# Attention and two quantised convolutions on 16 images: one more image through the filtered convolution, a reordered last head, split loads

## The chip, the cores and the metric

The kernel runs on one core of a Trainium2 chip. The metric is the device time of one execution in microseconds (us). All times are medians of repeated executions, and all comparisons use runs in the fast state (granted TensorE clock 0.994 in every profile of this study); five experiments have a single run each, whose state cannot be told, and are read by their profiles alone.

## The reference, cut to what matters

x is 16 images of 128 channels and 32 x 32 positions, in f32. Layer 0 is attention with 4 heads over the 1024 positions, layer 1 two 3x3 convolutions on values quantised to 4 bits, each followed by a batch norm over all images.

```python
# layer 0
scores = jnp.einsum('bnc,bcm->bnm', q, k) * c ** (-0.5)     # 64 heads of 1024 x 1024
attn = jax.nn.softmax(scores, axis=-1)
out = jnp.einsum('bnm,bmc->bnc', attn, v)
x = einsum(out, w_out) + b_out + x
# layer 1
out = act_quant(x)                       # round(clip(x, 0, 1) * 15) / 15
out = conv3x3(out, weight_quant(w1))
out = batchnorm(out, gamma1, beta1)      # mean and variance over (0, 2, 3): needs all 16 images
out = act_quant(out)
out = conv3x3(out, weight_quant(w2))
out = batchnorm(out, gamma2, beta2)
return out + x
```

The batch norms cut the program into stages: nothing of the second convolution can start before the last rows of image 15 have left the first, and no output before the last rows have left the second.

## The kernel before

Some names first. PSUM is the memory in which TensorE's products land; it is split into banks, and each buffer of `ps_s`, `ps_a` or `ps_m` takes up one or two. `u` (in PSUM `psu`) is an image multiplied by the folded query and key weights; `vo` (`psv`) is one multiplied by the folded value and output weights, which `fold_b` (`ps_b`) makes from wvo. `pad` is a quantised image with a border. The aggregate is the VectorE instruction that makes mean and variance out of the statistics of single tiles.

The loop of layer 0 has 512 steps: 64 heads (16 images of 4) with 8 chunks of 128 keys. A step does the scores of one chunk (`pss`, 4 records of 0.43 us), the exponential on ScalarE, and one step later the product with the values (`psa`). Other work is hung on steps by `at(step, function)`. The value projections of the next image (`psv`) stand at two steps of each head:

```python
vp = pool("vo", NCH + 4)          # 12 buffers for the projected values, 8 to an image
ps_s = pool("ps_s", 2, space=PSUM)
ps_a = pool("ps_a", 1, space=PSUM)   # tags a0 and a1
ps_m = pool("ps_m", 2, space=PSUM)   # tag "mm": u, v, filtered products, first conv
# ... in the loop of steps:
                if j in (5, 6) and b + 1 < B:
                    project_v(b + 1, 2 * h + j - 5)
```

The first convolution of images 0 to 13 runs inside this loop in a filtered form: the padded image is turned into 16 tiles of sums and differences, each is multiplied by a transformed weight (16 products of 256 columns, in place of 18 products of 512), and the results are summed. `products` does 4 of the 16. Images 14 and 15 are convolved directly after the loop:

```python
            if b < B - 2:
                at(end + 4, quantize, b, xt, A_LEVELS, 0.0)
                for i in range(2):
                    at(end + 5 + i, transform_rows, b, i)
                    at(end + 7 + i, transform_columns, b, i)
                    at(end + 14 + i, products, b, i)
                    at(end + 17 + i, transform_columns, b, 2 + i)
                    at(end + 22 + i, products, b, 2 + i)
                at(end + 26, statistics, b, 0)
# ...
        at(n_steps - 1, first_conv, B - 1, 0, RPH - 1, 0)
        at(n_steps + 1, normalise_group, len(GROUPS) - 1)
        for hf in range(NHF):
            at(n_steps + 2, first_conv, B - 2, hf * RPH)
        at(n_steps + 2, first_conv, B - 1, RPH - 1, 8, 1)
        at(n_steps + 3, first_conv, B - 1, RPH + 7, 9, 2)
```

A direct convolution writes one PSUM tile, which ScalarE copies out and VectorE takes statistics of, in this order:

```python
        ps = pool.tile([P, rows, W], F32, tag=tag, name=f"psc{n}_{b}_{r}")
        # ... nine products, one for each tap
        nc.scalar.copy(ys[b][:, r * W : (r + rows) * W], ps)
        if group is not None:
            nc.vector.bn_stats(place(n, b, group), ps)
```

## Time and profile before

| | before |
|---|---|
| time, first three runs | 2132.03 us (2131.83 to 2134.93) |
| span of the profiled execution | 2130.7 us |
| TensorE busy | 98% |
| first scores start | 10.11 us |
| loop: first scores to last scores | 2007.07 us |
| tail: last scores to the first aggregate of the batch norm | 15.08 us |
| first aggregate to the first product of the second conv | 4.21 us |
| second conv, to its aggregate | 65.03 us |
| aggregate to the first output pass | 1.99 us |
| first output pass to the end | 27.21 us |

The six stages and the start add up to the span. This is the way to read this kernel: TensorE is busy everywhere except at the joints, and each part of the change works at one joint. Intervals between two named instructions of one trace repeat to some hundredths of a microsecond in most stages (the loop to 0.3, the start and the output to less than that, as shown below), while whole runs differ by 2 us and more.

### The profile page before, as it was taken

To read this page: it belongs to the slowest core of one execution; us is meant where nothing else is said; L and a number is where in the kernel's file an instruction comes from. 1 tells how busy PE (TensorE), PEld (TensorE's weight loads), DVE (VectorE), ACT (ScalarE), POOL (GpSimd) and SP (SyncE) were. 2 spreads that over 40 slices of the span, in tenths; PEclk is the share of its full clock that TensorE was granted. 3 is DMA by queue.
4 is the path that set the end of the run, shared out by engine and by line. 5 is a ranking of instruction groups with operands and counts; after the bars stand their busy time and mean duration, and the time that the engine had idled before them with its cause. 6 is when DMAs were issued, how large, how long until landed. Compare 5 with 4: busy or idle time off the path is not lost.

```text
span 2130.7 us, 14771 instructions
## 1 busy us (share of the span) xinstructions
PE 2089.5 (98%) x5265; PEld 938.9 (44%) x5266; DVE 1445.9 (68%) x2139; ACT 735.7 (35%) x848; POOL 6.8 (0%) x16
## 2 busy tenths in 40 slices
PE   9999999999999999999999999999999999999994
PEld 4444444444444444444444444444444444444541
DVE  4776666767677676667758666775766667675676
ACT  2333333333333333333333333333333333333355
POOL 0000000000000000000000000000000000000000
PEclk9999999999999999999999999999999999999997
DMA  1000000000000000000000000000000000000043
GB/s 61 12 20 0 0 20 1 20 0 10 10 0 20 0 20 0 0 20 0 20 1 20 0 0 20 0 20 0 20 0 0 20 1 10 0 5 6 1 168 159
DMA packets 10609, 36.81 MB, mean 17 GB/s; under 512 B 1440, under 2 KB 1568, under 8 KB 10528
## 3 DMA queue, kind: packets, MB, share of 16 engines
q1 hardware_dynamic: 9872, 33.76, 4.3%
q10 hardware_dynamic: 656, 2.03, 0.3%
q8 instruction: 43, 0.70, 0.1%
q14 instruction: 38, 0.31, 0.0%
HBM read 19.01 MB, written 16.78 MB: 17 GB/s over the span
## 4 chain that ended last, share of the span: by engine, by line
PE 91%; DVE 7%; ACT 1%; issue 0%; DMA 0%; ACTq 0%; DVEq 0%
PE pss L480 38%; PE psa L504 37%; PE psv L459 5%; PE psu L448 5%; PE psc L275 3%; PE psw L711 1%; DVE rb L562 1%; DVE part L527 1%; DVE av L573 1%; DVE es L515 1%; DVE acc L574 1%; ACT e L493 1%; PE psa L619 1%; DVE y L856 1%; DVE side L553 0%; DVE vo L467 0%
## 5 line engine op out<-in xcount | busy, mean ns | idle before, releaser
L480 PE MATMUL pss<-u,x 128*128 128x512 f32 (+1 forms) x2064 | 964.7, 589 | 0.0
L493 ACT ACTIVATE e<-pss 128x1024 f32<-128x1024 f32 x511 | 522.8, 1023 | 1251.9 <-PE pss L480 1215.7
L504 PE MATMUL psa<-e,vo 128*128 128x512 f32 x2016 | 947.7, 592 | 0.0
L515 DVE TENSOR_TENSOR es<-es,e 128x1024 f32<-128x1024 f32 x378 | 461.2, 1220 | 366.4 <-ACT e L493 364.3
L480 PEld LDWEIGHTS pss<-u,x 128*128 128x128 f32 x2064 | 389.9, 190 | 474.1 <-issue 454.4
L504 PEld LDWEIGHTS psa<-e,vo 128*128 128x128 f32 x2016 | 379.4, 190 | 460.6 <-issue 459.4
L467 DVE COPY vo<-psv 128x512 f32<-128x512 f32 x128 | 88.2, 689 | 212.5 <-PE psv L459 212.5
L448 PE MATMUL psu<-x,at_sb 128*128 128x512 f32 x256 | 130.9, 593 | 0.3 <-DVE at_sb L414 0.2
L459 PE MATMUL psv<-bt_sb,x 128*128 128x512 f32 x256 | 130.4, 592 | 0.0
L527 DVE TRANSPOSE_TENSOR_REDUCE part<-es 128x32 f32<-128x1024 f32 (+1 forms) x66 | 80.6, 1221 | 2.2
L562 DVE STREAM_TRANSPOSE rb<-sums 128x1024 f32<-128x1024 f32 (+1 forms) x66 | 80.0, 1212 | 1.8
L513 DVE TENSOR_TENSOR es<-e,e 128x1024 f32<-128x1024 f32 x63 | 76.7, 1217 | 0.0
L459 PEld LDWEIGHTS psv<-bt_sb,x 128*128 128x128 f32 x256 | 48.6, 190 | 61.2 <-issue 61.0
L448 PEld LDWEIGHTS psu<-x,at_sb 128*128 128x128 f32 x256 | 48.4, 190 | 61.5 <-issue 53.8
L275 PE MATMUL psc<-pad,wq 128*128 128x512 bf16 (+3 forms) x333 | 71.9, 377 | 0.6 <-DVE pad L250 0.6
L453 DVE TENSOR_SCALAR u<-psu,au_sb 128x512 f32<-128x512 f32 x64 | 47.8, 746 | 34.2 <-PE psu L448 34.2
L718 ACT COPY wino<-psw 128x512 f32<-128x512 f32 x112 | 61.3, 589 | 24.9 <-PE psw L711 24.9
L703 DVE TENSOR_TENSOR tiles<-rows 128x1024 bf16<-128x1024 bf16 x56 | 67.1, 1219 | 0.5
L573 DVE TENSOR_TENSOR av<-av,rb 128x1024 f32<-128x1024 f32 x47 | 57.5, 1223 | 2.2 <-ACT e L493 0.3
L574 DVE TENSOR_TENSOR acc<-acc,av 128x1024 f32<-128x1024 f32 x47 | 57.3, 1220 | 0.5
L275 PEld LDWEIGHTS <-wq 128*128 128x128 bf16 x333 | 32.2, 97 | 39.9 <-DVE pad L250 1.1
L520 ACT COPY av<-psa 128x512 f32<-128x512 f32 x63 | 36.9, 585 | 37.2 <-PE psa L504 37.2
(121 smaller groups left out, 736.2 us busy)
## 6 DMA issues: line engine op xcount, KB each, us to landing
x_dram<-x SPq DMA_DIRECT2D x16, 512.0 KB, 2.6
res<-x_dram SPq DMA_DIRECT2D x16, 512.0 KB, 9.6
x<-in_x_dram SPq DMA_DIRECT2D x15, 512.0 KB, 3.6
out_dram<-y SPq DMA_DIRECT2D x15, 512.0 KB, 4.8
raw<-in_cw_dram ACTq DMA_DIRECT2D x2, 576.0 KB, 3.6
wvo_sb<-in_wvo_dram ACTq DMA_DIRECT2D x1, 514.0 KB, 6.8
out_dram<-y SPq DMA_DIRECT2D x2, 256.0 KB, 2.0
wqk_sb<-in_wqk_dram SPq DMA_DIRECT2D x1, 385.5 KB, 6.8
```

Of the source, the lines that this page charges most:

```text
L275: last = nc.tensor.matmul(ps, lhsT=wq[n][:, tap, :], rhs=pads[b % NPAD][:, r + dy : r + dy + rows, dx : dx + W], start=(tap == 0), stop=(t ...
L448: nc.tensor.matmul(ps, lhsT=at_sb[:, h, :], rhs=xt[b][:, ts(hf, HALF)], start=True, stop=True)
L459: nc.tensor.matmul(ps, lhsT=xt[b][:, ts(j, P)], rhs=bt_sb.rearrange("p h o -> p (h o)"), start=True, stop=True,)
L467: nc.vector.tensor_copy(vos[b, j], ps)
L480: last = nc.tensor.matmul(ps[:, ts(m, N // len(parts))], lhsT=xt[b][:, ts(key, P)], rhs=us[g][:, queries], start=True, stop=True,)
L493: exps[:] = [nc.scalar.activation(e, ps, AF.Exp).ins]
L504: nc.tensor.matmul(psa[g][m], lhsT=vos[b, j][:, ts(h, P)], rhs=e[:, ts(m, HALF)], start=(j == 0), stop=(j == NCH - 1),)
L515: added = nc.vector.tensor_tensor(es[g], es[g], es.pop((g, j)), ALU.add)
L527: nc.vector.tensor_reduce(part, total.rearrange("p (k c) -> p k c", c=Q), AX.X, ALU.add, apply_transpose=True,)
L562: nc.vector.transpose(rb, rinv.unsqueeze(2).to_broadcast([P, n, Q]))
L573: nc.vector.tensor_tensor(av, av, rb, ALU.mult)
L574: nc.vector.tensor_tensor(accs[b], accs[b], av, ALU.add)
```

## The change

The intent: run image 14 through the filtered form too, so that less is left after the loop; issue filtered products behind the scores of their step; put the last head's last products ahead of image 15's first rows; load what is needed first, first; and make the pieces at the start of each stage smaller, so that the next engine starts earlier. The diff, cut:

```diff
 # (start) the loads
-        nc.scalar.dma_start(out=wvo_sb, in_=wvo)
-        nc.sync.dma_start(out=wqk_sb[:, 1:], in_=wqk[:, 1:])
-        load(1)
+        nc.sync.dma_start(out=wvo_sb[0 : P // 2], in_=wvo[0 : P // 2])
+        nc.scalar.dma_start(out=wvo_sb[P // 2 :], in_=wvo[P // 2 :])
+        # load_rest: the rest of wqk, bo, bnp behind the first u; image 1 behind the first exponential
 # (conv) statistics ahead of the copy, and behind the last quantising
-        nc.scalar.copy(ys[b][:, r * W : (r + rows) * W], ps)
         if group is not None:
-            nc.vector.bn_stats(place(n, b, group), ps)
+            with tc.issue_after(after) if after else nullcontext():
+                nc.vector.bn_stats(place(n, b, group), ps)
+        nc.scalar.copy(ys[b][:, r * W : (r + rows) * W], ps)
 # (products)
+                with tc.issue_after(scored[0]):
                     for i in range(2):
                         nc.tensor.matmul(ps[:, i], lhsT=wino[:, l, k + i, :], ...)
 # (loop) image 14 filtered as well, with tighter slots
-            if b < B - 2:
+            when = (11, 13, 15, 19) if b == B - 2 else (14, 17, 22, 26)
+                at(end + when[0] + i, products, b, i)
+                at(end + when[1] + i, transform_columns, b, 2 + i)
+                at(end + when[2] + i, products, b, 2 + i)
 # (tail) image 14's direct convs gone, image 15's rows behind the last products
-        at(n_steps - 1, first_conv, B - 1, 0, RPH - 1, 0)
-            at(n_steps + 2, first_conv, B - 2, hf * RPH)
+        at(n_steps + 2, first_conv, 0, RPH - 1, 0)
+        at(n_steps + 2, first_conv, RPH - 1, 8, 1)
+        at(n_steps + 3, first_conv, RPH + 7, 9, 2)
 # (second conv) pieces of image 0's quantising, and of the first and last image's rows
-        for r0, r1 in ((0, RPH + 1), (RPH + 1, H)):
+        for r0, r1 in ((0, 10), (10, RPH + 2), (RPH + 2, H)):
+        starts = {0: (0, 8, RPH, H), B - 1: (0, RPH, H - 8, H)}
 # (output) quarters and halves first, the first two passes on VectorE
-            parts = NHF if b == 0 else 1
+        parts = {0: (0, N // 4, N // 2, N), 1: (0, N // 2, N), 2: (0, N // 2, N)}
+                if b == 0 and hi <= N // 2:
+                    nc.vector.tensor_scalar(y, y, scale2, bias2, ALU.mult, ALU.add)
```

More of the change, by code (lines that the diff above doesn't have):

```diff
@@ L222, in fast_path @@
     nc.gpsimd.memset(ones, 1.0)
-    LATE = 2
     STATS = nc.vector.BN_STATS_DIM
-    early = [keep.tile([P, (B - LATE) * NHF, STATS], F32, name=f"early{n}") for n in range(2)]
+    early = [keep.tile([P, (B - 1) * NHF, STATS], F32, name=f"early{n}") for n in range(2)]
     late = [
-        keep.tile([P, 3 + (LATE * NHF + 1 - n) * STATS], F32, name=f"late{n}") for n in range(2)
+        keep.tile([P, 3 + 3 * STATS], F32, name=f"late{n}") for n in range(2)
     ]
     for n in range(2):
-        nc.gpsimd.memset(late[n][:, 0:1], float((B - LATE) * N))
+        nc.gpsimd.memset(late[n][:, 0:1], float((B - 1) * N))
     ys = [keep.tile([P, N], F32, name=f"y{b}") for b in range(B)]
@@ L258, in place @@
     def place(n, b, i):
-        if b < B - LATE:
+        if b < B - 1:
             return early[n][:, b * NHF + i, :]
-        k = 3 + ((b - B + LATE) * NHF + i) * STATS
+        k = 3 + i * STATS
         return late[n][:, k : k + STATS]
@@ L266, in gather, with conv @@
         nc.vector.tensor_scalar(
-            late[n][:, 2:3], late[n][:, 2:3], float((B - LATE) * N), None, ALU.mult
+            late[n][:, 2:3], late[n][:, 2:3], float((B - 1) * N), None, ALU.mult
         )
-    def conv(pool, tag, b, n, r, rows=RPH, group=None):
+    def conv(pool, tag, b, n, r, rows=RPH, group=None, after=None):
         ps = pool.tile([P, rows, W], F32, tag=tag, name=f"psc{n}_{b}_{r}")
@@ L282, in conv @@
         ps = ps.rearrange("p h w -> p (h w)")
+        if group is not None:
+            with tc.issue_after(after) if after else nullcontext():
+                nc.vector.bn_stats(place(n, b, group), ps)
         nc.scalar.copy(ys[b][:, r * W : (r + rows) * W], ps)
-        if group is not None:
-            nc.vector.bn_stats(place(n, b, group), ps)
         return last
@@ L371, in fast_path, with load @@
         xt, us, vos, es, avs, psa, accs = {}, {}, {}, {}, {}, {}, {}
-        exps, sums_added, scored = [], [], []
+        exps, sums_added, scored, attended, quantized = [], [], [], [], []
         heads = [(b, h) for b in range(B) for h in range(NH)]
-        def load(b):
+        def load(b, queue=nc.sync):
             xt[b] = xp.tile([P, N], F32, tag="x", name=f"x{b}")
-            nc.sync.dma_start(out=xt[b], in_=x[b])
+            queue.dma_start(out=xt[b], in_=x[b])
         wqk_sb = once.tile([P, NH, 2 * P + 1], F32, tag="rows", name="wqk_sb")
@@ L386, in fast_path, with load_rest @@
         nc.scalar.dma_start(out=xt[0][:, ts(1, HALF)], in_=x[0][:, ts(1, HALF)])
-        nc.scalar.dma_start(out=wvo_sb, in_=wvo)
-        nc.sync.dma_start(out=wqk_sb[:, 1:], in_=wqk[:, 1:])
-        load(1)
-        nc.sync.dma_start(out=bo_sb, in_=bo)
-        nc.sync.dma_start(out=bnp_sb, in_=bnp)
+        nc.sync.dma_start(out=wvo_sb[0 : P // 2], in_=wvo[0 : P // 2])
+        nc.scalar.dma_start(out=wvo_sb[P // 2 :], in_=wvo[P // 2 :])
+        def load_rest(behind):
+            with tc.issue_after(behind):
+                nc.scalar.dma_start(out=wqk_sb[:, 1:], in_=wqk[:, 1:])
+                nc.scalar.dma_start(out=bo_sb, in_=bo)
+                nc.scalar.dma_start(out=bnp_sb, in_=bnp)
         def warm_up(n):
@@ L454, in project_u @@
             else:
-                nc.scalar.activation(dst, ps, AF.Identity, bias=au_sb[:, h : h + 1])
+                copied = nc.scalar.activation(dst, ps, AF.Identity, bias=au_sb[:, h : h + 1])
+                if g == 0:
+                    load_rest(copied.ins)
         def project_v(b, j):
@@ L544, in inverse_sums @@
                 for i in range(w):
-                    nc.tensor.matmul(
+                    product = nc.tensor.matmul(
                         ps, lhsT=quad, rhs=part[:, ts(i, n)], start=(i == 0), stop=(i == w - 1)
                     )
+                attended[:] = [product.ins]
                 nc.vector.reciprocal(rinv, ps)
@@ L614, in attend_group @@
             for m, key in enumerate(keys):
-                with tc.issue_after(first_product.ins) if final and m else nullcontext():
-                    if final and m == 1:
+                if final and m == 3:
+                    with tc.issue_after(attended[0]):
                         rbs[i] = inverse_sums(LAST, quadrant_sums(total), slice(*GROUPS[i]))
+                with tc.issue_after(attended[0]) if final and m else nullcontext():
                     product = nc.tensor.matmul(
@@ L625, in attend_group @@
                     )
-                first_product = first_product if m else product
+                attended[:] = [product.ins]
             avs[i] = psa[LAST, i]
@@ L639, in normalise_group @@
             done = quantize(b, x1, A_LEVELS, 0.0, cut.start // W, cut.stop // W)
+            quantized[:] = [done.ins]
             if i == len(GROUPS) - 1:
                 nc.sync.dma_start(out=x1d[b], in_=x1)
-                behind.append(done.ins)
         later = {}
@@ L709, in products @@
                 ps = ps_m.tile([P, 2, D, D], F32, tag="mm", name=f"psw_{b}_{l}_{k}")
-                for i in range(2):
-                    nc.tensor.matmul(
-                        ps[:, i],
-                        lhsT=wino[:, l, k + i, :],
-                        rhs=tiles[b][:, l % 2, k + i],
-                        start=True,
-                        stop=True,
-                    )
+                with tc.issue_after(scored[0]):
+                    for i in range(2):
+                        nc.tensor.matmul(
+                            ps[:, i],
+                            lhsT=wino[:, l, k + i, :],
+                            rhs=tiles[b][:, l % 2, k + i],
+                            start=True,
+                            stop=True,
+                        )
                 nc.scalar.copy(m[:, k : k + 2], ps)
@@ L731, in products, with first_conv @@
                     nc.vector.tensor_tensor(y[..., c], y[..., c], e, op)
-        def first_conv(b, r, rows=RPH, group=None):
-            convs[:] = [conv(ps_m, "mm", b, 0, r, rows, group).ins]
+        def first_conv(r, rows, group):
+            with tc.issue_after(attended[0]):
+                attended[:] = [conv(ps_m, "mm", B - 1, 0, r, rows, group, quantized[0]).ins]
         def keep_clock():
@@ L740, in keep_clock @@
             flat = wq[0].rearrange("p t o -> p (t o)")
-            with tc.issue_after(convs[0]):
-                for _ in range(21):
+            with tc.issue_after(attended[0]):
+                for _ in range(16):
                     nc.tensor.matmul(
@@ L750, in preload, with load_second @@
             nc.scalar.activation(keep.tile([P, 1], F32, name="unused"), last[:, N - 1 :], table)
+        def load_second():
+            with tc.issue_after(exps[0]):
+                load(1, nc.scalar)
         def late_bn_constants():
@@ L754, in late_bn_constants @@
                 bn_constants()
-        behind, convs = [], []
-        def late_statistics():
-            with tc.issue_after(behind[0]):
-                statistics(B - 2, 0)
         n_steps = len(heads) * NCH
+        at(1, load_second)
         at(NCH + 4, lambda: constants(cleared.ins, sums_added[0]))
@@ L769, in fast_path @@
             at(end + 6, sums_range, b)
-            if b < B - 2:
-                at(end + 4, quantize, b, xt, A_LEVELS, 0.0)
-                for i in range(2):
-                    at(end + 5 + i, transform_rows, b, i)
-                    at(end + 7 + i, transform_columns, b, i)
-                    at(end + 14 + i, products, b, i)
-                    at(end + 17 + i, transform_columns, b, 2 + i)
-                    at(end + 22 + i, products, b, 2 + i)
-                at(end + 26, statistics, b, 0)
-            else:
-                at(end + 4, quantize, b, xt, A_LEVELS, 0.0)
-        at((LAST - 2) * NCH, gather, 0)
+            at(end + 4, quantize, b, xt, A_LEVELS, 0.0)
+            when = (11, 13, 15, 19) if b == B - 2 else (14, 17, 22, 26)
+            for i in range(2):
+                at(end + 5 + i, transform_rows, b, i)
+                at(end + 7 + i, transform_columns, b, i)
+                at(end + when[0] + i, products, b, i)
+                at(end + when[1] + i, transform_columns, b, 2 + i)
+                at(end + when[2] + i, products, b, 2 + i)
+            at(end + when[3], statistics, b, 0)
+        at(LAST * NCH - 2, gather, 0)
         for i in range(len(GROUPS) - 1):
             at(LAST * NCH + FIRST_STEP[i + 1] + 1, normalise_group, i)
-        at(n_steps - 1, first_conv, B - 1, 0, RPH - 1, 0)
         at(n_steps - 1, preload, AF.Sqrt)
         at(n_steps + 1, normalise_group, len(GROUPS) - 1)
-        for hf in range(NHF):
-            at(n_steps + 2, first_conv, B - 2, hf * RPH)
-        at(n_steps + 2, first_conv, B - 1, RPH - 1, 8, 1)
-        at(n_steps + 2, late_statistics)
-        at(n_steps + 3, first_conv, B - 1, RPH + 7, 9, 2)
+        at(n_steps + 2, first_conv, 0, RPH - 1, 0)
+        at(n_steps + 2, first_conv, RPH - 1, 8, 1)
+        at(n_steps + 3, first_conv, RPH + 7, 9, 2)
         at(n_steps + 3, keep_clock)
@@ L832, in fast_path @@
             x1.append(t)
-        for r0, r1 in ((0, RPH + 1), (RPH + 1, H)):
+        for r0, r1 in ((0, 10), (10, RPH + 2), (RPH + 2, H)):
             quantize(0, ys[0], scale1, bias1, r0, r1)
         quantize(1, ys[1], scale1, bias1)
+        starts = {0: (0, 8, RPH, H), B - 1: (0, RPH, H - 8, H)}
         for b in range(B):
-            for hf in range(NHF):
-                conv(ps_c, "c", b, 1, hf * RPH, group=hf if b == B - 1 else None)
+            rows = starts.get(b, (0, RPH, H))
+            for i, (r0, r1) in enumerate(zip(rows, rows[1:])):
+                conv(ps_c, "c", b, 1, r0, r1 - r0, group=i if b == B - 1 else None)
             if b + 2 < B:
@@ L845, in fast_path @@
                     check_sums()
-            if b == B - LATE - 1:
+            if b == B - 2:
                 gather(1)
         scale2, bias2 = bn_params(1)
+        parts = {0: (0, N // 4, N // 2, N), 1: (0, N // 2, N), 2: (0, N // 2, N)}
         for b in range(B):
-            parts = NHF if b == 0 else 1
-            for i in range(parts):
-                cut = ts(i, N // parts)
-                y = ys[b][:, cut]
-                nc.scalar.activation(y, y, AF.Identity, bias=bias2, scale=scale2)
-                nc.vector.tensor_tensor(y, y, x1[b][:, cut], ALU.add)
-                nc.sync.dma_start(out=out[b][:, cut], in_=y)
+            ends = parts.get(b, (0, N))
+            for lo, hi in zip(ends, ends[1:]):
+                y = ys[b][:, lo:hi]
+                if b == 0 and hi <= N // 2:
+                    nc.vector.tensor_scalar(y, y, scale2, bias2, ALU.mult, ALU.add)
+                else:
+                    nc.scalar.activation(y, y, AF.Identity, bias=bias2, scale=scale2)
+                nc.vector.tensor_tensor(y, y, x1[b][:, lo:hi], ALU.add)
+                nc.sync.dma_start(out=out[b][:, lo:hi], in_=y)
     outer.close()
```

## The prediction

> **What bounds the kernel now.** I read the page first, then the engines' windows, TensorE's list of waits, and the timeline of the first 24 us and of everything after 2000 us.
>
> ```profile
> PE 2089.5 (98%) x5265; PEld 938.9 (44%) x5266; DVE 1445.9 (68%) x2139; ACT 735.7 (35%) x848; POOL 6.8 (0%) x16
> ...
> PE 91%; DVE 7%; ACT 1%; issue 0%; DMA 0%; ACTq 0%; DVEq 0%
> ```
>
> TensorE is busy for 98% of the span and carries 91% of the chain that ended last. So time can come from two places only: columns that TensorE no longer streams, and the few stretches where it idles or does filler work. The windows say where those are:
>
> ```profile
> 0.00:10.00 10.00, 6.67 (x22) 4.35 (x23) 1.11 (x3) 1.97 (x2) 3.73 (x12) 1.00 0.74 255
> 500.00:1000.00 500.00, 498.35 (x1202) 221.58 (x1201) 343.57 (x500) 167.92 (x194) 0.00 (x0) 1.00 0.03 9
> 2100.00:2131.00 31.00, 0.11 (x1) 0.00 (x0) 20.77 (x25) 19.46 (x19) 0.00 (x0) 0.56 0.67 272
> ```
>
> (First number after the stretch: its length; second: TensorE busy.) The 500 us in the middle lose 1.65 us. The first 10 us lose 3.3, the last 31 nearly all. What TensorE waited for:
>
> ```profile
> PE psw L711 <- DVE vo L467: 6.6, 14, 0.5
> PE ps_b L420 <- DMA wvo_sb<-in_wvo_dram: 1.9, 1, 1.9
> ```
>
> The first is 0.47 us once for each of 14 filtered images: a product waits for a buffer that VectorE still copies out. The second is the start.
>
> **What the skill says, and whether the trace agrees.**
> - "TensorE: Matmul & The Clock Gate", Back-to-back issue gap: N/2.4 + 2.5 ns when warm. Four filtered products of 256 columns stand 0.43 us from the next group (204.80 to 205.24), 0.11 each; the formula's 0.109 agrees. An f32 product costs four times a bf16 one here: 512 columns take 0.86 us (two products, shown as four records, per 1.72 us).
> - "VectorE: DVE Perf Modes", What auto-detection actually checks: a one-source SBUF operation runs two elements a cycle only if the outermost dimensions are both even, or equal. It agrees: below, 17 image rows into the padded image took 0.72 us and 15 rows 0.66, while 16 rows took 0.43 and 32 rows 0.70.
> - "PSUM — Partial Sum Buffer", PSUM bank collisions: two engines may not touch one bank together, reads included, so they are ordered. It agrees: the statistics of a PSUM tile start only when ScalarE's copy of it ends.
> - "DMA: Bandwidth & Descriptors", Queues, rings and completion order: the DMA engines alternate between the two issuing engines' queues. It agrees: 514 KB of wvo alone on one queue needed 6.8 us to land, beside 385 and 512 KB on the other.
>
> **The change, part by part.** Times are on the clock of the profile before; negative is faster.
>
> 1. *Start.* These lines are the end of the loads:
>
> ```profile
> 7.24 0.69 ACT L455 ACTIVATE u<-psu,au_sb 128x512 f32<-128x512 f32 x1 [1.04 <-PE psu L448]
> 9.14 1.13 PE L420 MATMUL ps_b<-wvo_sb 128*128 128x128 f32 x8 [1.94 <-DMA wvo_sb<-in_wvo_dram]
> ```
>
> wvo is split over both queues; the 385 KB of other weights and image 1 move behind u. Landing shows about 0.7 us after the last bytes (x's first half landed at 4.65; the 0.39 MB up to it had moved by 3.9). So wvo's bytes were through near 8.3, and the one-us windows (181, 231, 330, 367, 384, 388, 308 GB/s from 2.0 us on) sum to 1.97 MB by then, of which fold_b needed 1.18: the first weights, image 0 and wvo. Those 1.18 MB are through near 6.3 when nothing else is queued, and land at 7.0 to 7.4. The product before it leaves TensorE near 6.95, so fold_b starts at 7.2: -1.9. But the order of the new kernel puts the scores of step 1 ahead of both psv products, which now stand next to each other, and the fold after them needs a buffer that VectorE frees 0.7 us after the first: +0.2. Estimate -1.7.
>
> 2. *Products behind the scores.* The instruction order on TensorE is identical for images 0 to 13: the products were already behind the scores of their step. The 6.6 us stay: 0.
>
> 3. *Image 14 filtered.* 16 products of 256 columns more, at 0.1075: +1.72, inside the loop where TensorE is the bound. VectorE gets some 17 us more over steps 486 to 501, with slots packed tighter. I walked its order with the durations of the list of groups (1.22 for a sum of 1024, 0.69 and 0.42 for the filter's sums): at the change of heads in the middle of it the copy of av comes some 1.5 us later than in other heads, and about 0.5 us before the next product wants its buffer. 0.
>
> 4. *The tail.*
>
> ```profile
> 2019.28 2.02 PE L275 MATMUL psc<-pad,wq 128*128 128x480 bf16 x9
> ...
> 2025.03 6.26 PE L275 MATMUL psc<-pad,wq 128*128 128x512 bf16 x36
> ...
> 2031.33 0.40 ACT L283 COPY y<-psc 128x288 f32<-128x288 f32 x1 [0.75 <-PE psc L275]
> 2031.76 0.47 DVE L285 BATCH_NORM_STATS2 late<-psc 128x6 f32<-128x288 f32 x1 [0.72 <-ACT y L283]
> 2032.26 0.30 DVE L311 BATCH_NORM_AGGREGATE mv<-late 128x2 f32<-128x33 f32 x1
> ```
>
> x36 is 18 products of image 14 (3.9 us) and 18 of image 15. Image 14's go. In the new order the last products of the last head follow the scores directly: four keys 2019.28 to 2021.0, three more to 2022.3. Then TensorE waits for VectorE's part (2022.61 plus 0.2), 0.4 of sums, 0.43 of last product: 2023.55. Image 15's rows take 1.82 + 0.97 + 1.09: 2027.43. Meanwhile VectorE normalises and quantises the last quarter, 1.9 us of it after the last product: done at 2026.1, just before the last rows want it (2026.34). Statistics no longer wait for ScalarE's copy: aggregate at 2028.2 instead of 2032.26. -4.0.
>
> 5. *Smaller first quantised piece.*
>
> ```profile
> 2035.21 0.44 DVE L249 TENSOR_SCALAR qt<-qt 128x544 f32<-128x544 f32 x1 [0.91 <-ACT qt L248]
> 2035.69 0.72 DVE L250 TENSOR_SCALAR pad<-qt 128x544 bf16<-128x544 f32 x1
> 2036.33 0.40 DVE L249 TENSOR_SCALAR qt<-qt 128x480 f32<-128x480 f32 x1
> 2036.45 2.37 ACT L248 ACTIVATE qt<-y,bias,scale 128x1024 f32<-128x1024 f32 x2 [0.59 <-DVE pad L250]
> ```
>
> 10 rows for 17: ScalarE 0.66 to about 0.48, VectorE 0.44 to 0.33, and, rows now even, 0.72 to 0.33. -0.68. The later pieces come 0.3 to 0.4 us ahead of their conv.
>
> 6. *Second conv's end.*
>
> ```profile
> 2100.15 0.58 ACT L283 COPY y<-psc 128x512 f32<-128x512 f32 x1 [1.34 <-PE psc L275]
> 2100.77 0.70 DVE L285 BATCH_NORM_STATS2 late<-psc 128x6 f32<-128x512 f32 x1 [1.23 <-ACT y L283]
> ```
>
> Statistics start 0.58 earlier and cover 256 columns (0.43 for 0.70): -0.84.
>
> 7. *Output.* The first transfer leaves 1.6 us after the bias; now two passes of 256 on VectorE (0.30 + 0.42), so 0.8 earlier. But from 2108 on the transfers run at 373 to 422 GB/s until 2127, four us behind VectorE. The small pieces feed 131 KB per 0.72 us, less than that rate, and half-images add at 0.70 per 256 KB, so most of the 0.8 is starved away: by my count of bytes -0.3.
>
> Sum: -1.7 + 1.72 - 4.0 - 0.68 - 0.84 - 0.3 = -5.8, from 2132.0: **2126.2 us**, 0.27%.
>
> **Rivals.**
> - *The 6.6 us go as well* (the title suggests it): 2119.6. The unchanged order speaks against it.
> - *VectorE falls behind in image 14's packed steps.* It is 68% busy overall and nearly full at 2000 to 2005 (4.96 of 5). If av or a filtered tile comes late, TensorE stalls 0.5 to 2 us: 2127 to 2128.
> - *Image 14's rows were cover.* They hid the last normalising; my margin without them is 0.2 us. A wait at the last rows would cost up to 1: 2127.
> - *Half a transfer per queue is no faster.* If 64 partitions reach only half the engines' rate, or three issues on ScalarE delay bt, the start gives 0.7 rather than 1.7: 2127.2.
> - *Output wholly bound by the transfers' start*: all 0.8 kept: 2125.7.
>
> **Range and chances.** Three of the rivals add about a us each; two subtract, the larger of them unlikely. Repeats of the kernel before differ by up to 3.1 us (2131.83 to 2134.93), though two of three agree in 0.2. 80%: 2123.5 to 2129.0. A move of 2% (43 us) has no source in 98% busy TensorE: faster 0.005, slower 0.005, within 0.99.
>
> **What would show it.** The profile after should have: fold_b near 7.2 without a wait over 0.3; the psw waits on vo still 14 times 0.47; 240 psw records against 224; no new TensorE wait between 1950 and 2000; last rows right behind the others, and the first conv's aggregate about 4 us nearer to the last scores; 10-row quantising near 0.33; VectorE's last statistics ahead of ScalarE's copy; and the span from the bias to the end shorter by 0.2 to 0.8. I am wrong if the psw waits vanish, if TensorE waits for pad or av, or if the end does not move with the tail.

## The result, and the profile after

| | before | after |
|---|---|---|
| median of 4 runs | 2132.21 us | 2128.36 us (2127.49 to 2129.32) |
| ratio | | 0.9979, 95% interval 0.9962 to 0.9997 |
| span of the profiled execution | 2130.7 us | 2125.7 us |

A ratio here is the mean time of one kernel's fast runs over that of the other's of the same rounds, so it is not quite the ratio of the medians. The change saves 0.2%: within 2%, as predicted, and 2.2 us above the predicted time. Stage by stage, in the profiles:

| stage | before | after | difference | predicted |
|---|---|---|---|---|
| first scores start | 10.11 | 8.80 | -1.31 | -1.7 |
| loop | 2007.07 | 2008.83 | +1.76 | +1.72 |
| tail | 15.08 | 11.86 | -3.22 | -4.0 |
| aggregate to second conv | 4.21 | 3.46 | -0.75 | -0.68 |
| second conv to its aggregate | 65.03 | 64.19 | -0.84 | -0.84 |
| aggregate to output pass | 1.99 | 1.97 | -0.02 | |
| output | 27.21 | 26.59 | -0.62 | -0.3 |
| span | 2130.7 | 2125.7 | -5.0 | -5.8 |

The list of what TensorE waited for, after (total us, times, longest; two lines left out, 1.1 for the first operands and 0.5 for `pad` at the start of the second convolution, which the kernel before has as well):

```profile
PE psw L719 <- DVE vo L472: 6.6, 14, 0.5
PE psc L273 <- ACT y L284: 0.6, 1, 0.6
PE ps_b L423 <- DMA wvo_sb<-in_wvo_dram: 0.5, 1, 0.5
PE psu L451 <- DMA x<-in_x_dram: 0.4, 1, 0.4
```

The first line is that of the kernel before, unchanged: the products "behind each step's scores" still wait 14 times, and image 14, the fifteenth filtered image, does not. The wait for wvo has shrunk from 1.9 to 0.5, at the price of 0.4 for x. The second line is new: a convolution waits for ScalarE's copy. The timeline of the kernel after shows where (start, duration, then the work; in brackets the idle time before it and what ended it):

```profile
2019.72 3.27 PE L626 MATMUL psa<-e,vo 128*128 128x256 f32 x14
2024.09 3.03 PE L273 MATMUL psc<-pad,wq 128*128 128x480 bf16 x18
2026.37 1.22 DVE L283 BATCH_NORM_STATS2 late<-psc 128x6 f32<-128x480 f32 x2
2027.06 0.94 ACT L284 COPY y<-psc 128x480 f32<-128x480 f32 x2 [4.18 <-DVE late L283]
2027.67 1.29 PE L273 MATMUL psc<-pad,wq 128*128 128x288 bf16 x9 [0.55 <-ACT y L284]
2028.99 0.47 DVE L283 BATCH_NORM_STATS2 late<-psc 128x6 f32<-128x288 f32 x1 [1.40 <-PE psc L273]
2029.49 0.25 DVE L310 BATCH_NORM_AGGREGATE mv<-late 128x2 f32<-128x21 f32 x1
2032.56 0.33 DVE L248 TENSOR_SCALAR pad<-qt 128x320 bf16<-128x320 f32 x1
2096.67 0.43 DVE L283 BATCH_NORM_STATS2 late<-psc 128x6 f32<-128x256 f32 x1 [0.55 <-PE psc L273]
2097.14 0.25 DVE L310 BATCH_NORM_AGGREGATE mv<-late 128x2 f32<-128x21 f32 x1
```

Read the first seven lines as a chain. The first conv tile is complete near 2026, but VectorE takes its statistics only at 2026.37, behind the last quantising; in this order ScalarE may copy the tile only behind the statistics, at 2027.06; and the third piece of image 15 (x9, 288 columns) needs the bank of the first, since "mm" has two. So it starts at 2027.67 instead of right behind the second piece. The eighth line is the small quantised piece (0.33, where 17 rows took 0.72), the last two the end of the second conv: the statistics no longer follow a copy, and the aggregate follows them at once.

### The profile page after: what moved, and what is told of

Same layout as the page of the kernel before. It is cut to its first block, busy times and chain, and to the rows that moved or that the text cites. A ratio compares the mean times of both kernels' runs of the same rounds, so it can differ in the third digit from the quotient of the medians.

```text
span 2125.7 us, 14843 instructions
## 1 busy us (share of the span) xinstructions
PE 2086.8 (98%) x5277; PEld 939.7 (44%) x5277; DVE 1459.2 (69%) x2171; ACT 739.4 (35%) x858; POOL 6.9 (0%) x16
## 4 chain that ended last, share of the span: by engine, by line
PE 91%; DVE 7%; ACT 1%; issue 0%; DMA 0%; ACTq 0%; DVEq 0%
PE pss L485 38%; PE psa L509 37%; PE psv L464 5%; PE psu L451 5%; PE psc L273 3%; PE psw L719 1%; DVE rb L568 1%; DVE part L532 1%; DVE av L579 1%; DVE es L520 1%; DVE acc L580 1%; ACT e L498 1%; DVE y L866 1%; PE psa L626 0%; DVE side L559 0%; DVE vo L472 0%
## 5 line engine op out<-in xcount | busy, mean ns | idle before, releaser
L726 ACT COPY wino<-psw 128x512 f32<-128x512 f32 x120 | 65.6, 589 | 24.9 <-PE psw L719 24.9
L710 DVE TENSOR_TENSOR tiles<-rows 128x1024 bf16<-128x1024 bf16 x60 | 72.0, 1220 | 1.1 <-PE psw L719 0.6
```

## The experiments

Each kernel was built from one of the two by the edit shown. "Tail", "loop" and so on are the stages of the table above. All results were correct.

### A third bank for the last rows

```diff
+            pool, tag = (ps_a, "a1") if group == 2 else (ps_m, "mm")
-                attended[:] = [conv(ps_m, "mm", B - 1, 0, r, rows, group, quantized[0]).ins]
+                attended[:] = [conv(pool, tag, B - 1, 0, r, rows, group, quantized[0]).ins]
```

> The changed kernel, with the last piece of image 15's rows in a PSUM bank of its own. Theory: in the changed kernel these rows waited 0.55 us for ScalarE's copy of the first piece, because only two banks serve three pieces and the copy now comes after the statistics. Then here the wait is gone, the first conv's aggregate comes 11.3 us after the start of the last scores instead of 11.86, and the span shrinks by 0.5 us. Rival: the rows are held by the quantised last quarter, or VectorE's chain of statistics sets the end anyway: then the wait moves to the pad, or the aggregate stays within 0.2 of 11.86.

Measured: tail 11.15 instead of 11.86, span 2125.0; 2128.50 us in 19 runs, ratio 0.9981 (0.9974 to 0.9988). The timeline of this experiment:

```profile
2024.05 4.16 PE L273 MATMUL psc<-pad,wq 128*128 128x480 bf16 x27
2028.74 0.25 DVE L310 BATCH_NORM_AGGREGATE mv<-late 128x2 f32<-128x21 f32 x1
```

All 27 products of image 15 now run as one group without a gap, and the aggregate comes 0.75 earlier on the clock, 0.71 measured from the last scores. The listed wait was 0.55. The rest, 0.16, is what a stall costs beside its idle time: the Trainium skill's page "TensorE: Matmul & The Clock Gate", section "Single matmul latency", puts about 166 ns of a warm product beside its columns, and "Back-to-back issue gap" gives products in a row N/2.4 + 2.5 ns, without that part. The records here end that much after the columns (the profile models these ends), so a wait of 0.55 hides a gap of 0.71: from the last product of the second piece to the first of the third it is 0.82 in the kernel after and 0.11 here. Not all of it stays: the joint behind it, from the aggregate to the second conv, took 3.55 instead of 3.46, and did so in all three kernels with this bank; why is open. In a median of runs 0.7 us is not to be seen: 2128.50 against 2128.36.

### Tight slots for all images

The filtered products of images 0 to 13 are moved from steps 14, 15, 22 and 23 behind an image's end to 11, 12, 15 and 16, as the change has it for image 14.

```diff
-            when = (11, 13, 15, 19) if b == B - 2 else (14, 17, 22, 26)
+            when = (11, 13, 15, 19)
```

> The changed kernel, with image 14's step schedule for the filtered products of all images (11, 13, 15, 19 steps instead of 14, 17, 22, 26). Theory: the 14 waits of 0.47 us come from two products meeting two projections for the next image that hold both buffers until the next head; the tighter schedule is through before them. Then the waits on vo go from 6.6 us to under 1 and the span shrinks by 5.5 to 6.6 us. Rival: VectorE is short of time, and the wait only changes its name (tiles, av or vo in other steps): then TensorE's idle time in the loop stays at 5 to 8 us and the span within 1.5 us.

Measured: loop 2000.05 instead of 2008.83, so -8.78; span 2117.7, 8.0 less and so more than expected; 2119.53 us in 4 runs (2119.36 to 2119.97), ratio 0.9939 (0.9922 to 0.9956). The list of TensorE's waits of this experiment is complete with these four lines:

```profile
PE psu L451 <- DMA x<-in_x_dram: 1.9, 2, 1.5
PE unread L401 <- POOL sums L222: 1.1, 1, 1.1
PE psc L273 <- ACT y L284: 0.5, 1, 0.5
PE psc L273 <- DVE pad L248: 0.5, 1, 0.5
```

The wait for `vo` is gone. Why it was there can be read in the timeline of the kernel before:

```profile
224.56 1.02 PE L459 MATMUL psv<-bt_sb,x 128*128 128x512 f32 x2
...
228.86 1.02 PE L459 MATMUL psv<-bt_sb,x 128*128 128x512 f32 x2
...
241.73 1.88 PE L480 MATMUL pss<-u,x 128*128 128x512 f32 x4
242.21 1.22 DVE L574 TENSOR_TENSOR acc<-acc,av 128x1024 f32<-128x1024 f32 x1
243.35 0.68 DVE L467 COPY vo<-psv 128x512 f32<-128x512 f32 x1
244.09 0.38 PE L711 MATMUL psw<-tiles,wino 128*128 128x256 bf16 x2 [0.47 <-DVE vo L467]
```

The two `psv` are the next image's fifth and sixth projections, at steps 5 and 6 of the third head. The 12 `vo` buffers are full (8 of this image, 4 of the next), so the projections stay in PSUM, in both "mm" banks, until the fourth head has used the first values of this image: the copy out runs at 243.35, and the first bank was held from 224.56 to 244.03, 19.5 us. These values were used by 241.89, where the last of the products with them ends, but VectorE did the update of `acc` (242.21 to 243.43) ahead of the copy: of the 19.5 us the last 1.5 are VectorE's order, more than the wait itself. A copy ahead of `acc` was not tried. The filtered products at that time are the first to ask for an "mm" bank again. The scores' four records issue at 0.43 each until 243.45, and the next product at 244.09: a gap of 0.64, listed as 0.47. Fourteen images at 8.78 / 14 = 0.63 each fit this, again 0.16 above the listed wait. Issuing the products behind the scores does nothing against it; leaving the stretch in which the projections hold the banks does. Another way, 14 `vo` buffers, did not fit the memory and was never run.

### Image 14's filtering alone

The kernel before with image 14 filtered in the slots of the change, its 18 direct products in the tail taken out, its statistics taken with those of the other filtered images, and nothing else but the number of unread filler products behind the last rows (`keep_clock`, 16 for 21).

```diff
-    LATE = 2
+    LATE = 1
-            if b < B - 2:
+            when = (11, 13, 15, 19) if b == B - 2 else (14, 17, 22, 26)
-        for hf in range(NHF):
-            at(n_steps + 2, first_conv, B - 2, hf * RPH)
-                for _ in range(21):
+                for _ in range(16):
```

> The kernel before, with only image 14 filtered and its two direct convs taken out of the tail (and its statistics with the others). Theory: +1.76 us in the loop; 3.9 us of TensorE work leave the tail, but they covered the last normalising: the last rows now wait about 1.1 us for the pad. The first conv's aggregate comes 12.2 us after the start of the last scores instead of 15.08, and the span is 1.1 us shorter than before. Rival: no cover was needed, no wait on the pad over 0.3: aggregate near 11.2, span 2.2 shorter. Second rival: the packed steps stall TensorE on VectorE, and the loop costs 2.5 or more instead of 1.76.

Measured: loop 2008.77 (+1.70), tail 12.44 (-2.64), span 2129.4, so -1.3; 2131.35 us in 12 runs, ratio 0.9996 (0.9987 to 1.0004). TensorE's waits in this experiment:

```profile
PE psw L711 <- DVE vo L467: 6.5, 14, 0.5
PE psc L275 <- DVE pad L250: 2.8, 2, 1.7
```

The second line is two waits. The longest, 1.7, is at the start of the second convolution, where the kernel before waits 0.6: with fewer fillers the idle time there begins earlier, and the stage itself is no longer (4.15 against 4.21). The other is in the tail:

```profile
2028.92 1.28 PE L275 MATMUL psc<-pad,wq 128*128 128x288 bf16 x9 [1.16 <-DVE pad L250]
```

Image 14 took 3.9 us of TensorE in the tail and costs 1.7 in the loop, 2.2 less. But only 2.64 of the 3.9 left the tail, because the last rows now wait 1.16 for `pad`, for the last quantising: image 14's rows had been cover for it. This is the third rival of the prediction, in the order of the kernel before. The new order and the statistics ahead of the copy take off another 0.58 (12.44 to 11.86), and the third bank 0.71 more.

### Image 15's first rows ahead of the last products again

The kernel with the third bank, and the first 15 rows of image 15 back at the place that they had before.

```diff
+        def first_rows():
+            conv(ps_m, "mm", B - 1, 0, 0, RPH - 1, 0, quantized[0])
+        at(n_steps - 1, first_rows)
-        at(n_steps + 2, first_conv, 0, RPH - 1, 0)
```

> The changed kernel with the extra bank (third_bank), but the first 15 rows of image 15 again between the last scores and the last head's products, as before the change. Theory: the products end 1.3 to 1.5 us later, the normalising after them too, and only part is bought back by rows already done: the last rows wait about 1 us for the pad and the aggregate comes 11.7 to 12.0 us after the last scores instead of 11.15. Rival: the order is indifferent since TensorE has the same work: 11.1 to 11.3.

Measured (one run, 2127.54 us): tail 12.06 against 11.15, just above the expected range, and in its timeline the last rows wait:

```profile
2027.63 1.28 PE L273 MATMUL psc<-pad,wq 128*128 128x288 bf16 x9 [1.22 <-DVE pad L248]
```

The order is worth 0.9 once the bank is free: the rows that need no waiting fill the time of the last normalising only when they stand behind the last products.

### The copy ahead of the statistics again

```diff
+        nc.scalar.copy(ys[b][:, r * W : (r + rows) * W], ps)
         if group is not None:
             with tc.issue_after(after) if after else nullcontext():
                 nc.vector.bn_stats(place(n, b, group), ps)
-        nc.scalar.copy(ys[b][:, r * W : (r + rows) * W], ps)
```

> The changed kernel, with ScalarE's copy out of PSUM ahead of the statistics again. Theory: in the first conv the new order gains nothing, because the bank is then freed later and the last rows wait: here that wait goes from 0.55 to under 0.2 and the aggregate comes 11.7 to 12.0 us after the last scores (11.86 in the changed kernel); in the second conv, with six banks, the old order costs 0.5 to 0.6: from its start to its aggregate 64.7 to 64.8 instead of 64.19. Rival (my prediction): both ends lose, the first aggregate comes 0.4 or more later than 11.86.

Measured (one run, 2129.31 us): tail 12.09 against 11.86, second conv 64.60 against 64.19. The signs are those of the theory; the sizes are a little outside the expected ones: the tail is just above its range, the second conv 0.1 below, and the last rows still wait 0.35 where less than 0.2 was expected. The second conv's 0.41 is the copy of 256 columns (0.37) that stands ahead of the statistics again. The tail's 0.23 is a balance of two terms, the second of which its timeline shows:

```profile
2027.31 0.56 ACT L281 COPY y<-psc 128x480 f32<-128x480 f32 x1 [3.27 <-PE psc L273]
2028.62 1.28 PE L273 MATMUL psc<-pad,wq 128*128 128x288 bf16 x9 [0.35 <-DVE late L284]
```

The last copy (0.40 for 288 columns) is ahead of the last statistics, which loses 0.4; but the first copy starts when its tile is complete, and the first bank comes back sooner: the last rows wait 0.35 instead of 0.55. So only 0.2 of the wait comes from the new order, in which the first reader stands behind the quantising; 0.35 stays with either order, because two readers, one after the other (0.56 and 0.67 here), hold one of two banks. Statistics first is right for the last tile of a stage and slightly wrong for the one whose bank is wanted next; with the third bank this conflict does not arise.

### Nine rows in place of ten

```diff
-        for r0, r1 in ((0, 10), (10, RPH + 2), (RPH + 2, H)):
+        for r0, r1 in ((0, 9), (9, RPH + 1), (RPH + 1, H)):
```

> The changed kernel, with the first quantised pieces of 9, 8 and 15 rows instead of 10, 8 and 14. Theory (odd row counts drop VectorE to one element a cycle): the last pass of the 9 rows takes 0.46 us, longer than the 10 rows' 0.33, that of the 15 rows 0.66, and the second conv starts 0.07 to 0.12 later after the bias in spite of fewer rows. Rival: time goes with the rows: 0.31 and 0.42, conv 0.05 earlier.

Measured (one run, 2129.55 us): first aggregate to second conv 3.54 instead of 3.46, although there is less to do. The timeline of this experiment has the two pieces of image 0 that now have an odd number of rows, 9 and 15:

```profile
2034.38 0.46 DVE L248 TENSOR_SCALAR pad<-qt 128x288 bf16<-128x288 f32 x1
2036.14 0.66 DVE L248 TENSOR_SCALAR pad<-qt 128x480 bf16<-128x480 f32 x1
```

Nine rows take 0.46 where ten take 0.33 (2032.56 above), 15 rows 0.66 where 14 take 0.40 in the kernel after. So a good part of what this pass gained (0.72 to 0.33) is the even row count, and not the smaller piece.

### The output's pieces as before

```diff
-        parts = {0: (0, N // 4, N // 2, N), 1: (0, N // 2, N), 2: (0, N // 2, N)}
+        parts = {0: (0, N // 2, N)}
-                if b == 0 and hi <= N // 2:
+                if False:
```

> The changed kernel, with the output of the kernel before: two halves of image 0 through ScalarE, every other image whole. Theory: the end follows the first transfer one for one, so from the second bias to the end 27.2 us as before, instead of 26.6. Rival (the count of bytes in my prediction): the small pieces starve the transfers, and only 0.3 comes back: 26.9.

Measured (one run, 2129.97 us): output stage 27.29 against 26.59. That is what the first theory said. But the stage is less steady than the others: with the pieces of before it was 27.21, 27.11, 27.29 and, in a later profile, 26.68; with those of the change 26.55 to 26.72, and once 26.95. The gain is 0.4 us in the mean of these four and ten profiles, and one profile of each could have shown anything from -0.3 to 0.7; so this run alone does not decide against the 0.3 of the count of bytes.

### Two other splits of wvo

By heads, each half with all 128 partitions:

```diff
-        nc.sync.dma_start(out=wvo_sb[0 : P // 2], in_=wvo[0 : P // 2])
-        nc.scalar.dma_start(out=wvo_sb[P // 2 :], in_=wvo[P // 2 :])
+        nc.sync.dma_start(out=wvo_sb[:, 0:2], in_=wvo[:, 0:2])
+        nc.scalar.dma_start(out=wvo_sb[:, 2:4], in_=wvo[:, 2:4])
```

> The changed kernel, with wvo split over the two queues by heads (128 partitions each) instead of by partitions (64 each). Theory: the half of the partitions is what made the start gain 1.3 instead of 1.7 us: the last window of that load moved 245 GB/s at a full DMA share. Then fold_b starts at 7.3 or earlier instead of 7.84 and the loop's start is 0.5 us earlier. Rival: the bytes were through by 6.2 either way and the rest is the time from the last byte to the landing: fold_b starts at 7.7 to 7.9.

Not split at all, on ScalarE's queue:

```diff
+        nc.scalar.dma_start(out=wvo_sb, in_=wvo)
```

> The changed kernel, with wvo as one transfer of 128 partitions on ScalarE's queue behind the second half of image 0, as before the change; the other loads stay late. Theory: being alone is what matters, and nothing now stands between the two halves of image 0: the second half lands by 6.0 and wvo by 7.0, fold_b starts between 7.1 and 7.7 (later only if TensorE runs its first u at half rate, as in three of six profiles so far). Rival: both queues are needed: wvo lands after 7.6 and fold_b starts after 7.9.

Measured: by heads wvo landed 4.4 and 4.5 us after its issues, in place of 5.2 to 6.3 with the halves by partitions, and yet the first scores started at 8.73 against 8.80 (2127.21 us in 12 runs, ratio 0.9974, 0.9966 to 0.9983). Whole, it landed 4.7 after its issue and the first scores started at 8.05, the earliest of the study (2127.66 us in 10 runs, ratio 0.9975, 0.9966 to 0.9985). So half a transfer per queue was no faster than the whole in these profiles, as one rival had it (a later profile of the whole one differs, see the last experiment). The better transfer by heads did not show either, because something else had moved: fold_b started at 7.74, the rival's number, though wvo had landed at 6.75. Here is the same group in three kernels, first after:

```profile
5.06 2.28 PE L451 MATMUL psu<-x,at_sb 128*128 128x512 f32 x4 [0.40 <-DMA x<-in_x_dram]
7.84 1.13 PE L423 MATMUL ps_b<-wvo_sb 128*128 128x128 f32 x8 [0.49 <-DMA wvo_sb<-in_wvo_dram]
```

Then the kernel with wvo by heads:

```profile
4.82 3.06 PE L451 MATMUL psu<-x,at_sb 128*128 128x512 f32 x4 [0.17 <-DVE at_sb L417]
```

And the kernel with wvo whole:

```profile
4.79 1.98 PE L450 MATMUL psu<-x,at_sb 128*128 128x512 f32 x4 [0.27 <-DVE au_sb L417]
```

The same four records take 1.98 or 3.06: single records are 592 to 697 ns in some executions, up to 1222 in others. The Trainium skill's page "TensorE: Matmul & The Clock Gate", section "What's actually happening", has an idle array at half its clock, released only after a window of some 3.4 us of work whose phase is free, so that the same kernel differs from run to run. The trace agrees in the factor (1222 against 592 to 697); that the phase of this window is the cause no run here shows. With the loads of before a slow u is hidden behind the wait for wvo (1.9 us): the kernel with image 14 alone has u records of 1222 and 961 ns and starts its scores at 9.97. With wvo early a slow u is on the path.

### The loads alone, and the warm-up products taken out

The kernel before with the loads of the change and nothing else (the first block of the diff above):

> The kernel before with the change's loads alone. Theory: the loads' gain of 1.3 us in the one profile holds only when TensorE is already at full rate for u; with u at half rate the first scores start at 9.9 to 10.6, no earlier than before (10.0 to 10.1, where wvo was waited for and hid it). Over many runs the gain is then 0.3 to 0.8 us: ratio 0.9996 to 0.9999. Rival (my prediction): 1.3 to 1.7 us in every run, ratio 0.9992 to 0.9994.

Measured: first scores at 9.24 (before 10.11), span 2129.3; 2131.31 us in 13 runs, ratio 0.9994 (0.9986 to 1.0002). The interval holds both theories' numbers: it decides nothing between them. The profile fits neither: u ran at full rate (592 to 697 ns a record), and the gain was still only 0.87, because wvo landed 6.0 and 6.1 after its issues.

The kernel after without the three warming products ahead of the first weights:

```diff
-        warm_up(3)
```

> The changed kernel without the three warming products at the start. Theory (TensorE's rate at the start makes the spread between runs): u runs at half rate, its matmul records last about 1.2 us instead of 0.6 to 0.7, and the first scores start at 9.9 to 10.7 instead of 8.8. Rival (only the landings vary): records of 0.6 to 0.7 and first scores at 8.7 to 9.5.

Measured (one run, 2127.87 us): u at half rate, 3.60 us for the four records, as expected, but the first scores at 9.05 and not at the expected 9.9 to 10.7. Without the warming the first weights are multiplied at once (3.33 in place of 3.80), and wvo had landed when u was through. So the half rate of u alone does not cost the start its gain. Over the eight profiles with the change's split of wvo at this point of the study, the first scores came at 8.55 to 10.63, mean 9.46; with the loads of before at 10.11 and 9.97. The start's gain is thus about 0.6 in the mean, anything from -0.6 to +1.5 in one execution, and the records say what went with the late ones. In the three latest (9.92, 10.30, 10.63) all records of u take 1.06 us or more, and at least the first four of the eight of fold_b 0.42 in place of 0.27 (wvo landed 5.6 to 6.3 us after its issues). In the next two (9.24, 9.52) all are at full rate, but wvo landed 6 us after its issues, and in the later one x's second half 6.3 after its own (3.9 at best). What makes one execution start slowly stays open.

### The parts that gained, together

Tight slots for all images, the third bank and wvo whole:

> The changed kernel with the three edits that paid so far: the tighter schedule of the filtered products, a bank of its own for the last rows, wvo as one transfer on ScalarE's queue. Theory (the stages are independent): from the first scores to the last 2000.05 us as with the schedule alone, from the last scores to the aggregate 11.15, the rest as in the changed kernel: span 2116 to 2118, time 2117 to 2120. Rival (they interfere): a wait for a buffer or for VectorE comes back in the loop, span over 2119.

Measured: loop 2000.05, tail 11.16, span 2118.1; 2119.48 us in 5 runs, ratio 0.9935 (0.9922 to 0.9949). The two gains add without disturbing each other. wvo whole landed 6.9 us after its issue this time, not 4.7, and fold_b waited for it until 9.29, so that the first scores came at 10.25, later than in the kernel before; that is why the span is just over the expected one, and a gain of wvo whole is not shown. In time this kernel is not to be told from the tight slots alone (2119.53); both beat the changed kernel by 8.8 to 8.9 us.

## Why the prediction was right or wrong

The time was predicted 2126.2 and measured 2128.36, inside the range; within 2%, as nearly certain from the start. The 2.16 between them are made of three parts. The sum of the steps was -5.8 and the profiles show -5.0: 0.8. The medians differ by 3.85 and not by 5.0, because the profiled execution after was the fastest of its four (2127.49) while the one before took 2132.61: 1.15. And the median before had moved from 2132.03 to 2132.21 with a fourth run: 0.2. The prediction took a difference of two profiles for one of two medians. The range held with some luck: the start and the tail fell short by 0.4 and 0.8, and 0.3 more than predicted at the output hides part of it. A start that varies by 2 us, as above, would spread the runs after like this; the runs were not profiled one by one, so that is argued only.

1. *Start.* Predicted -1.7, profile -1.31. The term that failed is the landing: 0.7 after the last bytes was taken from x, and wvo needed 1.0 to 1.5 (bytes through near 6.2, landings at 7.2 and 7.7); x came 0.3 late as well. The 0.2 added for a buffer did not come: no such wait is in the list. And the 6.8 us of wvo, taken as agreeing with queues that alternate, shows only that the loads share the engines; no run here shows the turns. The greater error was to give one number at all: the other profiles put the gain at 0.6 in the mean.
2. *Products behind the scores.* Predicted 0, and 0 it was: 6.6 us in 14 waits before and after. The comparison of the instruction orders decided it against the title. What the prediction did not see is that the slots that it called packed for image 14 take the wait away for every image, and so that the change left 8.8 us where they were.
3. *Image 14 filtered.* Predicted +1.72, measured +1.76. The 240 products came without a new wait in image 14's steps, so VectorE did not fall behind.
4. *The tail.* Predicted -4.0, measured -3.22. The step that failed is "Image 15's rows take 1.82 + 0.97 + 1.09": it sums the three pieces without a gap. TensorE reached them on time (2024.09 after, 0.45 of it from the earlier stages, so 2023.64 on the clock of the prediction, which had 2023.55), and the quantising was in time too. But three pieces share two banks, and the first bank comes back only behind both of its readers, the statistics and the copy. The third bank showed this term at 0.71; the new order of the two readers is 0.2 of it. The prediction had looked for waits on `pad` and `av`, on data, and not for one on a buffer; "image 14's rows were cover" came true in the old order (a wait of 1.16 us) and not in the new.
5. *Smaller first piece.* Predicted -0.68, measured -0.75, with the pass at the predicted 0.33; odd rows confirmed as dear. Some 0.05 of the 0.75 is not from the piece: with image 14 filtered the aggregate reads 21 values for 33, and the stage took 4.15 for 4.21 in that experiment alone.
6. *Second conv's end.* Predicted and measured -0.84. Undoing the order took 0.41 of it back, with a copy of 256 columns.
7. *Output.* Predicted -0.3, measured -0.62 in this pair of profiles and -0.4 in the mean of all. The count of bytes came out low in this pair, and over all the profiles it is not refuted: the transfers were in fact held below their rate early in the stage, at 340 to 357 GB/s from 2.6 to 8.6 us into it and near 400 to 410 after, and the end came earlier all the same.

## What to carry to other kernels

Before moving an instruction that waits for a buffer, ask who holds the buffer and since when: moving the product behind other work changed nothing, moving it out of the stretch in which two projections kept both banks (19.5 us for the first) gained 8.8 us. Work that is cut from a tail may have covered a chain; the cut pays only with a new order behind it, and the order of two readers of a PSUM tile also sets when its bank returns. And measure small changes by intervals between named instructions: most stages repeated here to 0.1 us (not the start and the output), while runs of one kernel differed by 2 to 5.

## What the Trainium skill lacked or had wrong

- "TensorE: Matmul & The Clock Gate": half rate at a start and its run-to-run change agree (1222 against 592 to 697 ns a record). It warns that a trace's clock events can be unreliable. Lacking: that the granted clock in a profile can read full in that stretch (1.00 over the first 9 and 10 us of the third-bank and changed kernels, with records at double length in the former), so that it must be looked for in the records.
- The same page gives the latency of a product and its overlap in a row, and it fits; neither it nor another page that this study used says that a wait as listed in a profile, whose ends are modelled, is then short by it: 0.47 listed and 0.63 gained per image, 0.55 listed and 0.71 gained in the tail.
- "DMA: Bandwidth & Descriptors": a fixed cost of about 2 us beside the bytes is given for the GpSimd path. Missing for transfers side by side at a start is how little one landing repeats: wvo whole 4.7 and 6.9 us after its issue, x's second half 3.9 to 6.3.
- "PSUM — Partial Sum Buffer": that engines must not share a bank agrees. Lacking is the consequence for two readers of one tile: the order that serves the second engine's result (-0.23 us in the tail) holds the bank longer here (a wait of 0.55 us against 0.35 in the other order).
- "VectorE: DVE Perf Modes" had nothing wrong: 9 rows 0.46 us, 10 rows 0.33.
